# The order of two transpose groups and two output products in a gated delta net with experts

## The chip, the cores and the metric

The kernel runs on one core of one Trainium2 chip. The metric is the device time of the whole program in microseconds, from the start of the program to its end. The core's engines are TensorE (PE in the profile, with its weight loads on a row of their own, PEld), VectorE (DVE), ScalarE (ACT), GpSimd (POOL) and SyncE (SP), which only issues transfers here. Each engine works through its own instructions in the order in which they stand. An instruction that needs another engine's result waits on a semaphore, and whatever stands behind it on the same engine waits too.

## What is computed

The reference is one block of a transformer: attention by a gated delta rule, and then a mixture of experts. The change touches the attention part only, and of that its end:

```python
mixed_qkvz = einsum('bsd,od->bso', x, W_qkvz)            # projection: q, k, v, z
qkv = silu(conv_4(concat(q, k, v)))                      # causal convolution, 4 taps
# per chunk of 64 tokens, 32 value heads of 128 features:
M = tril(k_beta @ k.T * decay, -1);  T = inv(eye + M)
attn = (q @ k.T) * decay;  v_new = T @ v_beta - (T @ k_cumdecay) @ state
core = (q * exp(g)) @ state + attn @ v_new;  state = ...
h = core * rsqrt(mean(core ** 2) + eps)
h = norm_w * h * silu(z)
out = einsum('bsf,df->bsd', h, W_out)                    # the output product
x = x + layernorm(out)
# then 32 routed and 2 shared experts on layernorm(x), top 6 per token
```

There are 4 sequences of 256 tokens with 256 features, 16 query and key heads, 32 value heads. All values are 32-bit floats.

## The kernel before

**Units and turns.** The attention is cut into 32 units: one unit is one query/key head with its two value heads (R = 2) for two of the four sequences (512 tokens, four tiles of 128 rows). Every unit goes through the same stages, each a Python generator: `weights` and `decays` load and prepare, `prepare` projects (matmuls `pj`, line 390), convolves on ScalarE and VectorE (lines 398 and 400), squares the transposed q and k (`ptn`, lines 419 and 421) and forms the masked products of keys with keys and queries (`pk`, lines 442 and 461, scaled into the tile `am` by lines 446 and 464), `blocks` inverts small diagonal blocks on VectorE for two units at a time, `solve` combines them to the inverse by 64x64 products (lines 579, 640 and 648), `gate` makes the factor from z (line 364), and `finish` applies the inverse (`pu`), forms the output (`po`), normalises it on GpSimd (lines 709 and 711) and multiplies with the output weights.

**What sets the order.** Each `yield` of a generator names the place of the next step: `at(turn, slot)` is `turn * 9 + slot`, counted from the unit's own start, and unit u starts at turn u. A heap takes the step with the smallest place from all generators, and the order in which steps are taken is the order of the instructions on PE, ACT, DVE and POOL. So in one turn of the machine the first half of `prepare` of unit u, the second half of `prepare` of u-1, `solve` of u-2 to u-4 and `finish` of u-4 and u-5 are interleaved. SP is not in the list of engines ordered so: the recording layer orders its transfers itself.

**The end of `finish`.** For each half x (the first or the second 128 rows of the two sequences) four transposes turn `hm` into the PSUM tile `pth` (line 743), ScalarE copies it to `hT` (line 744), four products with the output weights `wo` sum into `pp` (line 749), and VectorE adds `pp` to the accumulator `acc` (line 754 for the first head, line 756 for the others). These steps stand in the same turn as the projections `pj` of the unit five later: `pj` number i of that unit stands at slot 2i + 0.7, so at 0.7, 2.7, 4.7 and 6.7. The step that multiplies two half inverses stands at slot 1.8 (`pyl`, line 640) and 3.7 (`pdl`, line 648, whose result line 650 copies to `phi` by two ScalarE instructions). The first level of `solve` of another unit (`py` and `pyx`, line 579) stands at 3.8.

**PSUM.** There are eight banks, two for each of four tags. `pj` has two of its own, `ms` is shared by `ptn`, `pk`, `ptv` and `pz`, `iv` by the products of `solve`, and `rc` by `pth`, `pp`, `pdl`, `pu`, `pm` and `po`. A tile that takes a bank waits for the last reader of the tile that had it.

A reader needs four names for a turn: `pth_0`, `pth_1` and `pp_0`, `pp_1` are the two halves' transposes and products; `pk_0`, `pk_1`, `pk_2` the three key products, of which `pk_1` takes the bank of `pk_0` and so waits for line 446 on it (called `am_0` below); `pj_0` to `pj_3` the projections. All matmuls but the transposes are recorded as two passes each.

Of the kernel before, what the change touches and what calls it, by code (L numbers as in the profile page):

```python
# [31 lines left out]
def at(turn, slot):  # L32
    return turn * SLOTS + slot
# [30 lines left out]
def gated_delta_net_moe(  # L64
# [26 lines left out]
    def bank(tag, shape, name):  # L91
        return psum.tile(shape, F32, tag=tag, name=name)
# [559 lines left out]
    def finish(u):  # L652

        hq, bp = units[u]
        yield at(4, 5)
        sz, vp, am, qe, phi = (state[u][k] for k in ("sz", "vp", "am", "qe", "phi"))
        vb = vp.rearrange("p (b x) r e -> p b x r e", x=2)
        ut = u1.tile([P, 2, 2, R, HD], F32, tag="ut", name=f"ut_{u}")
        rt = u1.tile([P, 2, R, HD], F32, tag="rt", name=f"rt_{u}")

        hm = u1.tile([P, 2, 2, R, HD], F32, tag="hm", name=f"hm_{u}")
        zb = sz.rearrange("p (b x) r e -> p x b r e", x=2)
        qx = qe.rearrange("p (b x) -> p x b", x=2)
        os_ = u2.tile([P, 2, 2, R], F32, tag="os", name=f"os_{u}")
        junk = u1.tile([P, HD], F32, tag="junk", name=f"junko_{u}")

        def solution(x):
            pu = bank("rc", [P, 2, R, HD], f"pu_{u}_{x}")
            for b in range(2):
                for r in range(R):  # L670
                    nc.tensor.matmul(  # L671
                        pu[:, b, r, :],
                        phi[:, r * NL + 2 * b + x, :],
                        rt[:, b, r, :] if x else vb[:, b, 0, r, :],
                        start=True,
                        stop=True,
                    )
            nc.scalar.copy(ut[:, x], pu)

        pos = {}  # L680

        def output(x):
            po = bank("rc", [P, 2, R, HD], f"po_{u}_{x}")
            for b in range(2):
                for r in range(R):
                    nc.tensor.matmul(  # L686
                        po[:, b, r, :], am[:, r, b, x, :], ut[:, 0, b, r, :], start=True, stop=(x == 0)
                    )
                    if x:
                        nc.tensor.matmul(  # L690
                            po[:, b, r, :], am[:, r, b, 4, :], ut[:, 1, b, r, :], start=False, stop=True
                        )
            for b in range(2):
                for r in range(R):
                    nc.scalar.activation(  # L695
                        junk, po[:, b, r, :], AF.Square, accum_out=os_[:, x, b, r : r + 1]
                    )
            pos[x] = po

        def gated(x):  # L700
            nc.vector.tensor_tensor(hm[:, x], pos[x], zb[:, x], ALU.mult)  # L701

        def normed(x):
            rs = u2.tile([P, 2, R], F32, tag="rs", bufs=4, name=f"rs_{u}_{x}")
            nc.vector.scalar_tensor_tensor(  # L705
                rs, os_[:, x], 1.0 / HD, qx[:, x].unsqueeze(2).to_broadcast([P, 2, R]), ALU.mult, ALU.add
            )
            rsf = rs.rearrange("p b r -> p (b r)")
            nc.gpsimd.tensor_tensor(rsf, rsf, nhalf[:, : 2 * R], ALU.pow)  # L709
            hf = hm[:, x].rearrange("p b r e -> p (b r) e")  # L710
            nc.gpsimd.tensor_tensor(hf, hf, rsf.unsqueeze(2).to_broadcast([P, 2 * R, HD]), ALU.mult)

        solution(0)
        yield at(4, 6)
        pm = bank("rc", [P, 2, R, HD], f"pm_{u}")
        for b in range(2):
            for r in range(R):
                nc.tensor.matmul(  # L718
                    pm[:, b, r, :], am[:, r, b, 3, :], ut[:, 0, b, r, :], start=True, stop=True
                )  # L720
        for b in range(2):
            nc.vector.tensor_tensor(rt[:, b], vb[:, b, 1], pm[:, b], ALU.subtract)
        yield at(4, 7)
        output(0)
        yield at(4, 7.45)
        gated(0)
        yield at(4, 8)
        solution(1)
        yield at(4, 8.2)
        normed(0)  # L730
        yield at(5, 0)
        output(1)
        yield at(5, 0.45)
        gated(1)
        yield at(5, 0.95)
        normed(1)
        for x in range(2):
            yield at(5, 1 + 2 * x)
            hT = u2.tile([P, 2, R, P], F32, tag="hT", name=f"hT_{u}_{x}")
            pt = bank("rc", [P, 2, R, P], f"pth_{u}_{x}")  # L740
            for b in range(2):
                for r in range(R):
                    nc.tensor.transpose(pt[:, b, r, :], hm[:, x, b, r, :], ident)
            nc.scalar.copy(hT, pt)  # L744
            yield at(5, 2.6 + 2 * x)
            pp = bank("rc", [P, 2, D], f"pp_{u}_{x}")
            for b in range(2):
                for r in range(R):
                    nc.tensor.matmul(  # L749
                        pp[:, b, :], hT[:, b, r, :], state[u]["wo"][:, r, :], start=(r == 0), stop=(r == R - 1)  # L750
                    )
            a = acc[:, bp * NL : (bp + 1) * NL, :].rearrange("p (b x) d -> p x b d", x=2)[:, x]
            if hq == 0:
                nc.vector.tensor_copy(a, pp)
            else:
                nc.vector.tensor_tensor(a, pp, a, ALU.add)
# [253 lines left out]
    for u in range(len(units)):  # L1010
        for stage in [weights, decays, prepare, gate, finish, solve] + [blocks] * (u % 2):
            begin(at(u, 0), stage(u))
# [57 lines left out]
```

## Time and profile before

| | us |
|---|---|
| median of 3 runs (1438.08 to 1443.58) | 1441.14 |
| the profiled execution's own time | 1443.05 |
| its span | 1441.3 |
| PE matmuls busy | 1353.2 (94%) |
| DVE busy | 872.6 (61%) |
| ACT busy | 852.3 (59%) |
| POOL busy | 554.6 (38%) |
| line 749, `pp`, 512 matmul records | 126.7 |
| line 743, `pth`, 256 records | 40.0 |

The span is that of one profiled execution, and it lies within the times of the runs. Busy time of PE is counted from records whose ends are modelled, so 94% does not say that the array is full for 94% of the time; what it loses is seen in the starts of the matmuls, and in the idle time of the weight-load row. Attention takes the span to about 1100 us; the rest is experts.

### The profile page before, as it was taken

To read this page: it belongs to the slowest core of one execution; us is meant where nothing else is said; L and a number is where in the kernel's file an instruction comes from. 1 tells how busy PE (TensorE), PEld (TensorE's weight loads), DVE (VectorE), ACT (ScalarE), POOL (GpSimd) and SP (SyncE) were. 2 spreads that over 40 slices of the span, in tenths; PEclk is the share of its full clock that TensorE was granted. 3 is DMA by queue.
4 is the path that set the end of the run, shared out by engine and by line. 5 is a ranking of instruction groups with operands and counts; after the bars stand their busy time and mean duration, and the time that the engine had idled before them with its cause. 6 is when DMAs were issued, how large, how long until landed. Compare 5 with 4: busy or idle time off the path is not lost.

```text
span 1441.3 us, 29913 instructions
## 1 busy us (share of the span) xinstructions
PE 1353.2 (94%) x11655; PEld 891.6 (62%) x11655; DVE 872.6 (61%) x1854; ACT 852.3 (59%) x2086; POOL 554.6 (38%) x430
## 2 busy tenths in 40 slices
PE   5668999999999999999999999999899999999996
PEld 3335766677777777777777677776665544444443
DVE  4576786878687687869879686877522242232122
ACT  3657778777777777777778677777443222122121
POOL 1353554566544556655544566545511100000000
PEclk8779999999999999999999999999999999999998
DMA  3344434334252433534242343533434565555621
GB/s 117 121 98 95 99 70 105 74 86 106 72 132 73 98 79 81 120 80 112 71 111 69 92 100 75 134 72 75 84 97 107 138 161 135 151 156 144 158 81 35
DMA packets 310157, 146.41 MB, mean 102 GB/s; under 512 B 240780, under 2 KB 281150, under 8 KB 310018
## 3 DMA queue, kind: packets, MB, share of 16 engines
q1 hardware_dynamic: 310018, 144.51, 40.9%
q8 instruction: 93, 1.52, 0.5%
q14 instruction: 46, 0.38, 0.1%
HBM read 129.40 MB, written 15.06 MB: 100 GB/s over the span
## 4 chain that ended last, share of the span: by engine, by line
PE 66%; DVE 14%; ACT 8%; DMA 7%; issue 3%; POOL 1%; SPq 0%; POOLq 0%; ACTq 0%; DVEq 0%
PE ph L922 11%; PE py L942 11%; PE pj L390 9%; PE pp L749 6%; PE pz L364 4%; DVE c L400 4%; DMA db<-dd 4%; PE pu L671 3%; PE pd L579 3%; DMA diag<-db 3%; PE po L686 3%; DVE prod L542 3%; ACT junk L421 2%; PE pk L461 2%; PE pm L718 2%
## 5 line engine op out<-in xcount | busy, mean ns | idle before, releaser
L400 DVE SCALAR_TENSOR_TENSOR c<-pj,cw,c 128x510 f32<-128x510 f32 (+2 forms) x384 | 286.1, 745 | 122.4 <-ACT c L398 113.3
L709 POOL TENSOR_TENSOR rs<-rs,nhalf 128x4 f32<-128x4 f32 x64 | 66.6, 1040 | 492.4 <-DVE rs L705 309.6
L390 PE MATMUL pj<-xT,w 128*128 128x512 f32 x512 | 250.3, 613 | 3.6 <-DVE c L400 3.4
L925 ACT ACTIVATE h<-ph,b1s 128x512 f32<-128x512 f32 (+1 forms) x94 | 64.6, 687 | 242.9 <-PE ph L922 242.7
L922 PE MATMUL ph<-xT,we 128*128 128x512 f32 (+1 forms) x376 | 177.4, 594 | 3.0 <-ACT phi L624 1.3
L931 DVE TENSOR_TENSOR hg<-h,gb 128x512 f32<-128x512 f32 (+1 forms) x94 | 65.0, 693 | 186.3 <-ACT h L925 169.8
L942 PE MATMUL py<-hg,we 128*128 128x512 f32 (+1 forms) x376 | 176.4, 593 | 0.0
L398 ACT ACTIVATE c<-pj,cw 128x512 f32<-128x512 f32 x128 | 87.6, 686 | 139.7 <-PE pj L390 139.5
L587 POOL TENSOR_TENSOR e<-am,cst 64x1024 f32<-64x1024 f32 x64 | 151.4, 2366 | 2.4
L390 PEld LDWEIGHTS pj<-xT,w 128*128 128x128 f32 x512 | 96.2, 198 | 77.8 <-issue 73.7
L749 PE MATMUL pp<-wo,hT 128*128 128x256 f32 x512 | 126.7, 391 | 7.3 <-ACT hT L744 4.6
L942 PEld LDWEIGHTS py<-hg,we 128*128 128x128 f32 (+1 forms) x376 | 71.3, 190 | 90.5 <-issue 89.1
L749 PEld LDWEIGHTS pp<-wo,hT 128*128 128x128 f32 x512 | 96.4, 193 | 45.0 <-ACT hT L744 30.5
L364 PE MATMUL pz<-wz,xT 128*128 128x256 f32 x512 | 121.2, 380 | 0.0
L922 PEld LDWEIGHTS ph<-xT,we 128*128 128x128 f32 (+1 forms) x376 | 69.6, 189 | 82.1 <-issue 78.1
L701 DVE TENSOR_TENSOR hm<-po,sz 128x512 f32<-128x512 f32 x64 | 43.7, 683 | 121.3 <-ACT junko L695 108.4
L346 POOL TENSOR_TENSOR gw<-gw,ng 128x512 f32<-128x512 f32 (+1 forms) x124 | 99.3, 832 | 2.4
L364 PEld LDWEIGHTS pz<-wz,xT 128*128 128x128 f32 x512 | 92.5, 190 | 10.5 <-issue 0.5
L191 POOL TENSOR_TENSOR rs_d<-rs_d,nhalf 128x2 f32<-128x2 f32 x4 | 2.8, 696 | 248.0 <-DVE rs_d L190 248.0
L446 DVE SCALAR_TENSOR_TENSOR am<-pk,br,gw 128x512 f32<-128x512 f32 x128 | 89.9, 744 | 6.7 <-ACT gw L338 4.8
L442 PE MATMUL pk<-c 128*128 128x512 f32 x128 | 74.6, 665 | 17.6 <-DVE am L446 10.5
L327 POOL TENSOR_TENSOR gw<-gw,cst 128x1024 f32<-128x1024 f32 x32 | 75.5, 2358 | 35.3 <-DMA gw<-g_rows 35.3
(188 smaller groups left out, 2768.7 us busy)
## 6 DMA issues: line engine op xcount, KB each, us to landing
gw<-g_rows SPq DMA_DIRECT2D x32, 768.0 KB, 6.5
w<-in_w_qkvz SPq DMA_DIRECT2D x32, 512.0 KB, 3.9
diag<-db SPq DMA_DIRECT2D x128, 128.0 KB, 3.4
we<-in_w SPq DMA_DIRECT2D x126, 128.0 KB, 3.0
gb<-gate_rows SPq DMA_DIRECT2D x34, 256.0 KB, 3.7
wz<-in_w_qkvz SPq DMA_DIRECT2D x32, 256.0 KB, 3.1
wo<-in_w_out SPq DMA_DIRECT2D x32, 256.0 KB, 2.7
mb<-am SPq DMA_DIRECT2D x64, 128.0 KB, 2.7
```

The source lines that it names most:

```text
L327: nc.gpsimd.tensor_tensor(gd, gd, neg.unsqueeze(1).unsqueeze(1).to_broadcast([P, 2 * R, 2, P]), ALU.add)
L346: nc.gpsimd.tensor_tensor(y, y, g.unsqueeze(2).to_broadcast([P, 2, n * P]), ALU.add)
L364: nc.tensor.matmul(pz[:, j].rearrange("p r e -> p (r e)"), xT[:, k, t * P : (t + 1) * P], state[u]["wz"][:, k, :], start=(k == 0), stop=(k ...
L390: nc.tensor.matmul(pj.rearrange("p b s -> p (b s)"), state[u]["w"][:, k, col * P : (col + 1) * P], xT[:, k, bp * T : (bp + 1) * T], start= ...
L398: nc.scalar.activation(y, pj, AF.Copy, scale=cw[:, row, 3:4])
L400: nc.vector.scalar_tensor_tensor(y[:, :, back:], pj[:, :, : S - back], cw[:, row, 3 - back : 4 - back], y[:, :, back:], ALU.mult, ALU.add,)
L442: nc.tensor.matmul(pk, s[:, 1, b * S : b * S + P], s[:, 0:2, b * S : (b + 1) * S], start=True, stop=True)
L446: nc.vector.scalar_tensor_tensor(am[:, r, b, 0:4, :].rearrange("p (i x) c -> p i (x c)", i=2), pk, br[:, 2 * b, r : r + 1], gw[:, r, b, 0: ...
L587: nc.gpsimd.tensor_tensor(e[g], mt[g, :, g].unsqueeze(1).to_broadcast(full), lev[g].unsqueeze(2).to_broadcast(full), ALU.mult,)
L749: nc.tensor.matmul(pp[:, b, :], hT[:, b, r, :], state[u]["wo"][:, r, :], start=(r == 0), stop=(r == R - 1))
L922: nc.tensor.matmul(ph[:rows], w[:, k * P : k * P + rows], xT[:, k, c], start=(k == 0), stop=(k == 1))
L942: nc.tensor.matmul(py[m], w[:rows, 2 * P + m * P : 2 * P + (m + 1) * P], hgs[i // 3][:rows, i % 3 * T : (i % 3 + 1) * T], start=False, sto ...
```

## The change

Two lines in `finish` change, both of them places.

```diff
         for x in range(2):
-            yield at(5, 1 + 2 * x)
+            yield at(5, 1 + 2.9 * x)
             hT = u2.tile([P, 2, R, P], F32, tag="hT", name=f"hT_{u}_{x}")
             pt = bank("rc", [P, 2, R, P], f"pth_{u}_{x}")
...
             nc.scalar.copy(hT, pt)
-            yield at(5, 2.6 + 2 * x)
+            yield at(5, 2.72 + 2.03 * x)
             pp = bank("rc", [P, 2, D], f"pp_{u}_{x}")
```

The first transposes stay at slot 1. The first product moves from 2.6 to 2.72, the second from 4.6 to 4.75; so each of them, with its addition to `acc`, stands behind the projection next to it (2.7 and 4.7) instead of ahead of it. The second transposes, with their copy, move from slot 3 to 3.9: behind `pdl` (3.7) and the first-level products `py` and `pyx` (3.8), and no longer ahead of `pk_1` (3.4). No instruction is added or taken away.

## The prediction

> **What bounds the kernel now.** I read the engines' shares first, then the waits, then one turn in order of time. The page says that TensorE is the busiest engine, and the chain that ended last runs mostly over it:
>
> ```profile
> PE 1353.2 (94%) x11655; PEld 891.6 (62%) x11655; DVE 872.6 (61%) x1854; ACT 852.3 (59%) x2086; POOL 554.6 (38%) x430
> PE 66%; DVE 14%; ACT 8%; DMA 7%; issue 3%; POOL 1%; SPq 0%; POOLq 0%; ACTq 0%; DVEq 0%
> ```
>
> The other third of the chain matters here: it passes through ACT and DVE at fixed places of each turn. The table of waits gives those near the change (total us, times, longest):
>
> ```profile
> PEld pp L749 <- ACT hT L744: 30.5, 30, 3.0
> PEld pdl L648 <- DVE acc L756: 17.4, 23, 0.8
> PEld pk L442 <- DVE am L446: 16.2, 27, 7.1
> PEld pth L743 <- POOL hm L711: 11.0, 29, 2.0
> PEld py L579 <- DMA diag<-db: 10.4, 15, 2.5
> ```
>
> So the moved instructions do wait in nearly every turn: products for their transposed operand, `pdl` for its bank (held by pp_0 until line 756 has read it), transposes for GpSimd, `pk_1` for am_0, and py for a transfer. A weight load runs one matmul ahead, so its idle time overstates what the array loses. That is read from one turn's order of time (start, duration, engine and line). ACT and DVE:
>
> ```profile
> 500.55 0.28 ACT L695 ACTIVATE junko<-po 128x128 f32<-128x128 f32 x1 [0.22 <-PE po L690]
> ...
> 503.61 0.68 ACT L398 ACTIVATE c<-pj,cw 128x512 f32<-128x512 f32 x1
> 504.19 0.58 ACT L744 COPY hT<-pth 128x512 f32<-128x512 f32 x1
> ...
> 511.37 0.75 ACT L650 COPY phi<-pdl 64x256 f32<-64x256 f32 x2 [0.17 <-PE pdl L648]
> ...
> 504.33 2.31 DVE L400 SCALAR_TENSOR_TENSOR c<-pj,cw,c 128x510 f32<-128x510 f32 x3 [1.49 <-ACT c L398]
> ...
> 507.23 0.86 DVE L643 TENSOR_SCALAR y_l<-pyl 64x256 f32<-64x256 f32 x2
> 508.12 1.41 DVE L446 SCALAR_TENSOR_TENSOR am<-pk,br,gw 128x512 f32<-128x512 f32 x2
> ```
>
> and TensorE, with the group at 509.58 being pk_1:
>
> ```profile
> 503.58 1.13 PE L442 MATMUL pk<-c 128*128 128x512 f32 x2
> 504.82 1.99 PE L749 MATMUL pp<-wo,hT 128*128 128x256 f32 x8
> 506.65 1.88 PE L390 MATMUL pj<-xT,w 128*128 128x512 f32 x4
> 508.37 0.60 PE L419 MATMUL ptn<-cst,c 128*128 128x128 f32 x4
> 508.97 0.66 PE L743 MATMUL pth<-cst,hm 128*128 128x128 f32 x4
> 509.58 1.13 PE L442 MATMUL pk<-c 128*128 128x512 f32 x2
> ```
>
> The reader is to see that pk_1 starts 0.05 us after am_0 ends (508.12 + 1.41 = 509.53), and that am_0 stands at the end of a chain without a hole: TensorE's po, ScalarE from 500.55 (four squares of po, four of ptn, the scaling at 503.61), VectorE from 504.33 to 509.53. Nothing in it comes from pth_0, pp_0 or pj_1. So **pk_1 is pinned** about 7.1 us behind pth_0, whatever TensorE does in between. This turn is typical: in 18 of the 23 turns from 280 us to 976 us pk_1 starts 7.13 to 7.15 us behind pth_0, and later in the others.
>
> **The change part by part.** The streaming times are the start-to-start distances of the trace: pk_0 takes 2 x 0.43 = 0.86 us, a pj group 4 x 0.43 = 1.72, a pp group 8 x 0.216 = 1.73, four transposes 0.44 and about 0.09 more where the kind of work changes.
>
> *The first product behind the projection.* Before, pk_0 has streamed by 503.58 + 0.86 = 504.44 and pp_0 starts at 504.82, because the copy of hT ends at 504.77: 0.38 us lost, some 0.28 of it more than a change of work costs. After, pj_1 fills that hole (504.45 to 506.17), pp_0 runs 506.17 to 508.0. This stall goes. What is late next: ptn_0 (to 508.45) and then pk_1, which still starts at 509.58. The 0.28 us, the 0.15 us that pth_1 waits for GpSimd and the 0.1 us of wait ahead of pk_1 are swallowed by the pin. **Gain up to pk_1: nothing.**
>
> *The second transposes behind pk_1.* They used 0.53 us of the time ahead of the pin, which was needed by nothing else. They now stand behind it, where TensorE has no spare time: before, from 509.58 to the next unit's pu at 516.13, its groups follow one another with only the 0.2 us hole ahead of pdl. **Cost: +0.53 us a turn.** TensorE now idles 508.45 to 509.58 instead.
>
> *pdl no longer waits for line 756.* In the built program pdl takes the bank of pth_0, free by 504.77, so it starts when pk_1 has streamed, 509.58 + 0.86 = 510.45 instead of 510.64: **-0.2 us a turn.**
>
> *A new wait.* In the built program pth_1 is given the very bank that pdl used just before it, and its first transpose waits for ScalarE too, where before it waited for TensorE and GpSimd alone. The releaser is line 650. Its two copies end 512.12 - 510.64 = 1.48 us after pdl's start, so after the change at 510.45 + 1.48 = 511.93. TensorE arrives earlier: pdl, py and pyx took 511.72 - 510.64 = 1.08 us, so 511.53. **Cost: +0.45 us** in turns like this one. ScalarE is free for line 650 in time: ptn_0 ends 0.4 us earlier than before, so the squares are done by about 510.4. Queued behind pth_1 on TensorE are pk_2, pj_2, pp_1 and pu, and the whole next turn. In the other turns (every second one) py waits 0.3 to 0.5 us for the diag transfer, whose landing does not move; there TensorE arrives about when line 650 ends, and the new wait costs about nothing.
>
> This is the place to weigh a rule. The row is 511.37 with 0.75 us for line 650. The Trainium skill, page "Perfetto Trace Analysis", section "Matmuls", says that independent matmul groups should go round different PSUM banks so that one's evacuation runs beside the next one's matmuls. pdl and pth_1 are independent and share a bank now; the rule speaks against this change. By the rule kept (other bank) a turn would cost 0.53 - 0.2 = +0.33 us; by the row +0.8. I take the row.
>
> *The second product behind the projection.* hT for it is ready: pth_1 ends about 512.5, the copy takes 0.58, and pk_2 (0.96) and pj_2 (1.72) come first. Before, py, pyx and pk_2 covered it as well. Zero either way; without that cover, the copy with its latency would cost about 0.8 us. VectorE does the same work in another order (the convolution of pj_1 ahead of the addition) without an idle gap from 504.33 to 517, so it is neither sooner nor later at pk_1's and py's results. po later takes pp_1's bank: line 756 is done about 518, po starts after 520. Zero.
>
> *SP and POOL.* The order of transfers changes with it: the load of wo (line 307), which waited for pp_1 at the head of SP's queue (released at 514.64), now stands behind the two mb stores (0.63 us of issue each) and in every second turn behind gw (about 0.6 to 1.0 us). The mb stores were issued at 516.61, when line 464 had ended, so they gain nothing. wo is issued about 518.5 at the latest and lands 2.7 us later, at about 521.2; POOL's scaling of it (line 312) started at 520.36, so it may slip by 1 us; POOL then has about 8 us idle, and wo is first used in the next turn. The load of wm stands behind wo, needs about 519.9 and finds wo issued by then. Zero; uncovered it would be 1 us a turn.
>
> **Sum.** Turn as shown: pth_1 at 511.98, pk_2 512.5, pj_2 513.5, pp_1 515.2, pu 516.9 instead of 516.13: +0.8. Turns with the diag wait: 0.53 and little else, +0.55. From the first unit's output to the last projection there are some 28 turns: 14 x 0.8 + 14 x 0.55 = 18.9 us. In the last four, without projections to hide the copy, pth_1 stands nearer to pp_1: about 0.6 us each, 2.4 us. Sum 21 us. Against the span of 1441.3 this gives 1462.6; the median, 1441.14, lies by the span, so I say 1462 for it. After 1160 us the experts keep TensorE full, so a late start is not won back.
>
> **The rivals.**
>
> *Displacement alone* (16%): the copy of line 650 comes soon enough, or the diag wait is in all turns, and only 0.33 us a turn remain: 29 x 0.33 = 10, so 1451. For it: the new wait is a difference of two times of about a microsecond. Against: the rows above.
>
> *A second circuit* (9%): pp_1 and its addition come 2.5 us later than before, and if VectorE's addition then holds up line 722 or po, or ScalarE (copy, silu, table load and exponentials in a row from 512.4) delays the convolution by 0.6 us, a turn costs 1.4: 28 x 1.4 = 39, so 1480. For it: ScalarE's row is dense there. Against: TensorE arrives later too.
>
> *Faster* (6%): pk_1 isn't pinned. If the chain to am_0 gains from TensorE's later turns, so that pk_1 follows ptn_0 at once (508.5), and TensorE doesn't wait for line 650, a turn gains 1.1 - 0.33 = 0.75: 28 x 0.75 = 21, so 1420. It decides from the point where am_0 ends 0.33 us earlier relative to pth_0 (0.8 if line 650 holds). Against: ScalarE waits 0.22 us for po at 500.55, so the chain starts from TensorE itself and moves with it.
>
> *No difference* (8%): the sum of pin and displacement cancels, for instance where GpSimd is late for pth_1 (2.0 us at the longest) and the later place hides it: 1441 to 1448.
>
> **How the numbers follow.** My case has 61%, alone within 1455 to 1472. Within 0.5% (7.2 us, about what a measurement of this kernel can tell from no change) lies only the fourth rival: 8%. Slower: 61 + 16 + 9 = 86%. Faster: 6%. The range leaves out the faster rival, most of no difference and the far end of the second circuit: 1448 to 1479.
>
> **What would show it.** Right: pp no longer waits for hT in most turns; pth waits for line 650 some 14 to 25 times, 0.4 us or more each; pdl no longer waits for line 756; pk's wait for line 446 rises to about 1 us a turn; a turn is 0.5 to 0.8 us longer between pk_1 and pu, and equal between pth_0 and pk_1. Wrong: pk_1 less than 6.9 us behind pth_0, or turns lengthened anywhere else.

## The result, and the profile after

The changed kernel takes 1467.79 us (median of 5 runs, 1462.45 to 1469.04) where the kernel before takes 1441.35 (5 runs, 1438.08 to 1444.46). The ratio is 1.0171, with an interval of 1.0152 to 1.0190: slower by 26 us, where 21 were forecast, and inside the range. The profiled execution took 1468.96 us. From its page, the span, the engines' shares and the chain that ended last:

```profile
span 1466.8 us, 29860 instructions
...
PE 1351.3 (92%) x11655; PEld 900.6 (61%) x11655; DVE 874.5 (60%) x1854; ACT 853.0 (58%) x2086; POOL 554.7 (38%) x430
...
PE 66%; DVE 11%; ACT 9%; POOL 7%; issue 3%; DMA 3%; SPq 0%; POOLq 0%; ACTq 0%; DVEq 0%
```

The matmuls, VectorE, ScalarE and GpSimd are as busy as before, to within 2 us; 25.5 us of span were added beside that. Where it waits is in the table of waits of the changed kernel (total us, times, longest; rows between are left out):

```profile
ACT phi L650 <- PE pdl L648: 43.8, 32, 3.1
PEld pk L442 <- DVE am L446: 43.7, 27, 7.5
PE pk L442 <- DVE am L446: 37.3, 27, 7.3
PEld pdl L648 <- issue: 21.1, 29, 0.8
PE pth L743 <- POOL gw L327: 6.4, 15, 0.4
PEld pp L749 <- ACT hT L744: 6.2, 6, 2.1
```

The products' wait for hT has gone from 30.5 us to 6.2, as the change intends. In its place TensorE's wait ahead of pk for line 446 has risen to 37.3 us in 27 waits. Before, its row was this:

```profile
PE pk L442 <- DVE am L446: 10.5, 7, 6.8
```

In both kernels one long wait (6.8 and 7.3 us) lies far ahead of the first output. After, the other 26 are pk_1's, in 26 of the 28 turns from the first output to the last projection; in the remaining two pk_1 waits for ScalarE's squares. pth has a wait in 15 turns. `pdl` is no longer booked to line 756, yet its weight load loses 21.1 us to "issue": the hole stayed, and only its name changed.

The turn that the prediction followed, in order of time (start, duration, engine, line; count; idle time before and its releaser). It starts with pth_0 at 510.29; the rows of `pyl`, `py` and `pyx`, and other rows of DVE and ACT, are left out:

```profile
510.29 0.60 PE L743 MATMUL pth<-cst,hm 128*128 128x128 f32 x4
511.43 1.13 PE L442 MATMUL pk<-c 128*128 128x512 f32 x2
512.40 1.88 PE L390 MATMUL pj<-xT,w 128*128 128x512 f32 x4
514.11 1.89 PE L749 MATMUL pp<-wo,hT 128*128 128x256 f32 x8
515.84 0.60 PE L419 MATMUL ptn<-cst,c 128*128 128x128 f32 x4
515.98 1.41 DVE L446 SCALAR_TENSOR_TENSOR am<-pk,br,gw 128x512 f32<-128x512 f32 x2
517.44 1.13 PE L442 MATMUL pk<-c 128*128 128x512 f32 x2 [1.00 <-DVE am L446]
518.50 0.51 PE L648 MATMUL pdl<-phi,y_l 64*64 64x64 f32 x10
519.22 0.75 ACT L650 COPY phi<-pdl 64x256 f32<-64x256 f32 x2 [1.12 <-PE pdl L648]
520.07 0.63 PE L743 MATMUL pth<-cst,hm 128*128 128x128 f32 x4 [0.43 <-POOL gw L327]
520.53 1.03 PE L461 MATMUL pk<-c 128*128 128x256 f32 x4
521.40 1.88 PE L390 MATMUL pj<-xT,w 128*128 128x512 f32 x4
523.12 1.89 PE L749 MATMUL pp<-wo,hT 128*128 128x256 f32 x8
524.84 1.05 PE L671 MATMUL pu<-vp,phi 128*128 128x128 f32 x8
```

The first projection (512.40) does fill the hole that pp_0 left, and TensorE is done with everything ahead of pk_1 at 516.4. It then idles for 1.00 us, because am_0 ends at 517.39, as pinned as before. Behind pk_1 stands what used to be ahead of it: pth_1, and in front of that 0.43 us of wait. The profile books the wait to GpSimd's line 327; but the two copies of line 650, which hold the bank that pth_1 takes, end at 519.22 + 0.75 = 519.97, and pth_1 starts 0.10 us later. It is a wait for several semaphores, and the engine named is not the one that matters. Measured from pth_0, in us, in a regular turn (before without the diag wait / with it; after the same in both kinds):

| | pk_1 | pdl | pth_1 | pk_2 | pp_1 | pu |
|---|---|---|---|---|---|---|
| before | 7.14 | 8.20 | 6.52 | 9.28 / 9.6 to 9.8 | 10.24 / 10.5 to 10.8 | 13.69 / 14.0 to 14.2 |
| after | 7.15 | 8.20 | 9.78 | 10.24 | 12.82 | 14.55 |

So up to `pdl` nothing has moved, and the turn is 0.86 us longer, or 0.3 to 0.6 where the diag transfer used to be waited for. Of the 25.5 us, 21.2 lie in the 28 turns from the first pth_0 on (902.7 against 881.5 us), 1.4 in what follows, and 2.9 ahead of the first output.

Not all of this is waiting. The profile also gives the granted clock, the share of its full clock at which TensorE could run. In the table of stretches (length, busy us of PE, PEld, DVE, ACT, POOL with counts, granted clock, DMA share, GB/s) the stretch from 100 to 150 us reads, before and then after:

```profile
100.00:150.00 50.00, 44.93 (x537) 31.14 (x529) 33.27 (x72) 35.10 (x85) 20.00 (x14) 0.95 0.39 86
```

```profile
100.00:150.00 50.00, 45.18 (x521) 32.37 (x514) 32.17 (x70) 33.32 (x71) 20.36 (x15) 0.88 0.34 87
```

No moved matmul has run by then, and TensorE's busy time is no less: its clock was granted at 0.88, not 0.95. The clock goes to half in pieces of some 3.4 us. From 112 to 1420 us the trace before has two of them (6.8 us in all), the trace after six and one of 10.2 us (30.7 in all). Two of those, at 126 and 146 us, go with the 2.9 us ahead of the first output. Four more fall into the turns that begin at 216, 668, 804 and 871 us, which are 1.7 to 2.2 us longer than before, and the one of 10.2 us into the turn at 1055, which is 2.6 longer. The one in the turn at 804 (second line), and the corresponding place of the kernel before (first line):

```profile
798.00:804.00 6.00, 4.68 (x47) 3.69 (x48) 5.05 (x11) 3.18 (x3) 5.85 (x7) 1.00 0.49 108
```

```profile
815.20:818.60 3.40, 3.40 (x38) 3.01 (x39) 1.27 (x3) 1.30 (x2) 3.40 (x4) 0.50 0.50 111
```

That is not an accident of one execution: the mean granted clock is 0.969 to 0.975 in the five runs after (median 0.972), and 0.973 to 0.982 in the 126 runs of the kernel before that stand beside the experiments (median 0.978). Among those 126, a run with 0.001 less took 0.9 to 1.2 us longer, so I estimate that 5 to 7 of the 26 us come by way of the clock. The kernels below with the transposes displaced have medians of 0.972 to 0.974, the others 0.975 to 0.981. What lowers the clock was not tried apart.

### The profile page after: what moved, and what is told of

It reads as the page before. It is cut to its first block, busy times and chain, and to the rows that moved or that the text cites. A ratio compares the mean times of both kernels' runs of the same rounds, so it can differ in the third digit from the quotient of the medians.

```text
span 1466.8 us, 29860 instructions
## 1 busy us (share of the span) xinstructions
PE 1351.3 (92%) x11655; PEld 900.6 (61%) x11655; DVE 874.5 (60%) x1854; ACT 853.0 (58%) x2086; POOL 554.7 (38%) x430
## 4 chain that ended last, share of the span: by engine, by line
PE 66%; DVE 11%; ACT 9%; POOL 7%; issue 3%; DMA 3%; SPq 0%; POOLq 0%; ACTq 0%; DVEq 0%
PE ph L922 11%; PE py L942 11%; PE pj L390 8%; PE pz L364 6%; DVE c L400 5%; PE pp L749 4%; PE pu L671 4%; PE po L686 4%; PE pd L579 4%; ACT junk L421 3%; POOL gw L327 3%; ACT junko L695 2%; PE pm L718 2%; PE pk L461 2%; PE po L690 2%
## 5 line engine op out<-in xcount | busy, mean ns | idle before, releaser
L749 PE MATMUL pp<-wo,hT 128*128 128x256 f32 x512 | 123.3, 384 | 3.6 <-ACT hT L744 3.6
L442 PE MATMUL pk<-c 128*128 128x512 f32 x128 | 75.0, 669 | 44.8 <-DVE am L446 37.3
L421 ACT ACTIVATE junk<-ptn 128x128 f32<-128x128 f32 x256 | 71.0, 277 | 49.3 <-PE ptn L419 42.2
L364 PEld LDWEIGHTS pz<-wz,xT 128*128 128x128 f32 x512 | 92.5, 190 | 10.5 <-issue 0.5
```

The source lines that it names most:

```text
L364: nc.tensor.matmul(pz[:, j].rearrange("p r e -> p (r e)"), xT[:, k, t * P : (t + 1) * P], state[u]["wz"][:, k, :], start=(k == 0), stop=(k ...
L421: nc.scalar.activation(junk, pt[:, t, :], AF.Square, accum_out=ss[:, i, t : t + 1])
L442: nc.tensor.matmul(pk, s[:, 1, b * S : b * S + P], s[:, 0:2, b * S : (b + 1) * S], start=True, stop=True)
L749: nc.tensor.matmul(pp[:, b, :], hT[:, b, r, :], state[u]["wo"][:, r, :], start=(r == 0), stop=(r == R - 1))
```

## The experiments

Each was timed in three rounds beside the kernel before (medians 1442.81 to 1443.74 us in those runs), so ratios are compared. "Behind pth_0" is read as in the table above. All compute the whole result.

**Each half of the change alone.** First the transposes alone:

```diff
-            yield at(5, 1 + 2 * x)
+            yield at(5, 1 + 2.9 * x)
```

> Only the second transposes move (slot 3 to 3.9); both products stay ahead of their projections. Theory of the pin: pk_1 stays about 7.1 us behind pth_0, since its bank comes free with line 446, and the transposes' 0.5 us are added behind it; here pth_1 takes the bank of pp_0 and need not wait for line 650, so a turn gets about 0.45 us longer and the run is 10 to 18 us above the kernel before: 1451 to 1459. Rival, that the products' new places cost the time: no more than 3 us above the kernel before. Rival, that the bank shared with pdl is the whole of it: also near the kernel before.

Measured: 1461.88 us (1459.86 to 1464.94), ratio 1.0126 [1.0095, 1.0157]; 3 us above what was expected. pk_1 stays at 7.14, pdl at 8.20, pth_1 stands at 9.28 (it waits for no bank here) and pu at 14.15, +0.46. The displacement alone brings the largest part of the loss. In its profile the 26 turns from the first pth_0 on took 16.9 us more than before; 8.6 of that lie in three turns in which the clock is at half for 3.4 or 6.8 us, and those had not been counted on.

Then the products alone:

```diff
-            yield at(5, 2.6 + 2 * x)
+            yield at(5, 2.72 + 2.03 * x)
```

> Only the two products move behind their projections; the second transposes stay at slot 3. Theory of the pin: the removed wait of pp_0 for its transposes (some 0.3 us a turn) gains nothing, because pk_1 still starts 7.1 us behind pth_0; pdl now takes the bank of pth_1 and may wait about 0.3 us for its copy: 1441 to 1449, not faster. Rival, that the removed wait is worth its own length: 27 x 0.3 = 8 us faster, 1433. Rival, that the products' places cost the time of the change: about 1462 to 1468.

Measured: 1448.02 us (1445.51 to 1454.82), ratio 1.0038 [1.0025, 1.0051]. The wait that the change aims at is gone and nothing was gained for it; the kernel is some 5 us slower. From the table of waits of this kernel:

```profile
PEld pp L749 <- ACT hT L744: 4.9, 4, 2.1
PEld pdl L648 <- ACT hT L744: 22.3, 25, 1.2
PEld pth L743 <- POOL hm L711: 22.2, 30, 2.0
```

pp_0 moves to 3.82 (from 2.38) and pk_1 stays at 7.14: the time goes into pth_1's wait for GpSimd, which grew from 11.0 to 22.2 us and is swallowed by the pin too. Here `pdl` takes another bank and waits for a copy of hT, 0.14 us longer than it waited before, and pu is at 13.83.

**The bank.** The changed kernel, with pth_1 in a bank of the projections, so that it shares none with `pdl` (in the units 0 to 25):

```diff
-            pt = bank("rc", [P, 2, R, P], f"pth_{u}_{x}")
+            pt = bank("pj" if x and u < 26 else "rc", [P, 2, R, P], f"pth_{u}_{x}")
```

> The changed kernel with the second transposes of the units 0 to 25 in a bank of the projections, so that they don't wait for line 650's copies of pdl. Theory: pth_1 starts right behind py and pyx, about 9.3 instead of 9.8 us behind pth_0 in turns without a wait for the diag transfer, 9.5 to 9.6 in the others: 0.2 to 0.5 us a turn, 6 to 12 us faster than the changed kernel, 1456 to 1462, and still 15 us or more above the kernel before, because the displaced transposes remain. Rival, that the shared bank is the whole loss: about 1443. Rival, that the bank costs nothing since the transfer would be waited for anyway: 1466 to 1469.

Measured: 1459.54 us (1458.01 to 1459.84), ratio 1.0106 [1.0078, 1.0134], about 9 us less than the changed kernel. Its timeline in the same turn (pth_0 at 505.80):

```profile
512.94 1.12 PE L442 MATMUL pk<-c 128*128 128x512 f32 x2 [1.00 <-DVE am L446]
...
514.73 0.75 ACT L650 COPY phi<-pdl 64x256 f32<-64x256 f32 x2 [1.12 <-PE pdl L648]
...
515.08 0.65 PE L743 MATMUL pth<-cst,hm 128*128 128x128 f32 x4
```

pth_1 starts at 9.28 while line 650 is still at work until 515.48, with no idle time in front of it. So the releaser was line 650, whatever the wait was booked to, and the wait cost 0.5 us in the turn. pk_1's 1.00 us of idling is as in the changed kernel, and the displaced transposes still stand behind it: the turn is 31.03 us, 0.39 longer than before. Of the rest of this kernel's loss, part is again in turns with the clock at half (three, 7.3 us).

**The pin.** The changed kernel, with the scaling of pj_0 (line 398) ahead of ScalarE's four squares of ptn_1, so that am_0's chain no longer holds these squares (about 0.4 us each), and TensorE's work is the same:

```diff
                 nc.tensor.transpose(pt[:, t, :], s[:, i, t * P : (t + 1) * P], ident)
+            if i:
+                yield at(1, 0.72)
             for t in range(NL):
...
-        squares(1)
+        yield from squares(1)
```

(and the same for the call of `squares(0)`, which yields nothing.)

> The changed kernel with ScalarE's scaling of pj_0 (line 398) ahead of its four squares of ptn_1 instead of behind them, so that VectorE's chain to am_0 begins about 0.9 us earlier. Theory of the pin: pk_1 starts about 6.2 instead of 7.15 us behind pth_0, and the turn gets up to 0.9 us shorter where nothing else holds it (where the diag transfer lands late, about 0.2): 12 to 22 us faster than the changed kernel, 1446 to 1456. Rival, that pk_1's start isn't what limits the turn: within 4 us of the changed kernel, 1464 to 1470.

Measured: 1450.02 us (1446.18 to 1453.24), ratio 1.0040 [1.0028, 1.0052]: a gain of 19 us, where the loss was 26, from an edit that touches no instruction of the change. Its timeline (lines are up to 2 further down; pth_0 at 503.55):

```profile
503.75 0.69 ACT L398 ACTIVATE c<-pj,cw 128x512 f32<-128x512 f32 x1 [0.53 <-PE pj L390]
...
508.26 1.41 DVE L448 SCALAR_TENSOR_TENSOR am<-pk,br,gw 128x512 f32<-128x512 f32 x2
...
509.73 1.12 PE L444 MATMUL pk<-c 128*128 128x512 f32 x2
```

The scaling now waits only for its projection and starts 0.20 us behind pth_0. am_0 starts 4.71 us behind pth_0 rather than 5.69 and ends at 509.67; pk_1 follows at 6.18 rather than 7.15, with no idle time of the array in its row. That is the pin: ScalarE's order sets the place of pk_1, and TensorE's order cannot.

Both repairs together (the two edits above on the changed kernel):

> The changed kernel with both repairs: the second transposes in a bank of their own and the scaling of pj_0 ahead of the squares. Theory: the two losses, pin and bank, are of different places and their repairs mostly add up (8 and 18 us alone): 1437 to 1446, at the kernel before. Rival: they are one loss, and both repairs together give no more than the larger alone, 1450.

Measured: 1442.77 us (1440.33 to 1448.63), ratio 0.9988 [0.9973, 1.0003]. The two gains, 9 and 19 us, add up to the loss. They do not undo it place by place: the regular turn is 30.06 us, where it was 30.64 before, the turns with the diag wait 31.0 to 31.5 rather than some 31.0, and the clock stays at 0.973. The earlier scaling alone on the kernel before was not run, so how much it would have gained there is not known. The nearest pair, with the products ahead of their projections and py moved in both, is at the end of the next part (before_py and before_early_py): there it brings 0.33%, about 5 us, and pk_1 does not come earlier (7.30 rather than 7.14). So I take most of the 19 us to be a matter of the changed order.

**The gain behind the pin.** If the products' place is good and only the pin hides it, it should show once the pin is lifted. First the products' move without its cost on VectorE: in it, line 756 stands behind the convolution, and here it is kept ahead of it.

```diff
             nc.scalar.activation(y, pj, AF.Copy, scale=cw[:, row, 3:4])
+            yield at(0, 2 * i + 0.76)
             for back in range(1, 4):
...
-            yield at(5, 2.6 + 2 * x)
+            yield at(5, 2.72 + 2.03 * x)
```

> Both products stand behind their projections on TensorE, the second transposes stay at slot 3, and VectorE keeps the old order (the addition of pp ahead of the convolution of the projection next to it), so that the banks go round as before and no new wait appears. Theory of the pin: the wait of pp_0 for its transposes (0.3 us a turn) is gone from the waits, pk_1 still starts 7.1 us behind pth_0, and the time stays that of the kernel before: 1438 to 1446. Rival, that the removed wait is worth its length once no new wait comes with it: 8 us faster, near 1435.

Measured: 1446.83 us (1443.71 to 1450.07), ratio 1.0027 [1.0017, 1.0037], just above the expected range. pdl is back at 8.20 and pu at 13.68 as before, in the regular turns. The profiled execution loses its 4 us in a few others: some with the clock at half (in the one with pu at 19.16 it is so for 6.8 us), some in which py waits longer for the diag transfer. With the pin in place, no gain.

The same with the earlier scaling:

> The kernel split with ScalarE's scaling of pj_0 ahead of its squares of ptn_1. Theory of the pin: am_0 ends 0.9 us earlier, pk_1 now starts when TensorE gets to it, about 6.6 us behind pth_0, and the removed wait counts: up to 0.5 us a turn, less where the diag transfer is waited for, 5 to 13 us faster than the kernel before, 1430 to 1438. Rival: TensorE's other work holds the turn anyway, 1440 to 1445.

Measured: 1439.00 us (1433.68 to 1445.53), ratio 0.9974 [0.9962, 0.9986], a little above the expected range. pk_1 is at 6.42 and pu at 12.86, but only in every second turn; in the others the diag transfer, which lands no earlier, now holds up py and all that stands behind it, and pu is mostly at 13.6 to 14.4.

So py and pyx were moved behind pk_2 as well:

```diff
-            yield at(3, 3.8 + 4 * i)
+            yield at(3, 3.8 + 4 * i) if i else at(3, 4.45)
```

> The kernel split_early with the first-level products of solve (py and pyx) behind pk_2 (slot 4.45 instead of 3.8), so that pk_2's 0.9 us lie before the wait for the diag transfer. Theory: the turns with that wait gain too, 0.5 us in nearly every turn, 10 to 20 us faster than the kernel before, 1424 to 1434. Rival: VectorE, which now does the sums of py and pyx behind the scaling of pk_2, is late for the next products, 1436 or more.

Measured: **1425.75 us** (1424.67 to 1427.38), ratio 0.9880 [0.9858, 0.9901]: faster than both kernels. Its timeline (lines up to 3 further down; pth_0 at 490.81):

```profile
496.79 0.60 PE L746 MATMUL pth<-cst,hm 128*128 128x128 f32 x4
497.23 1.02 PE L445 MATMUL pk<-c 128*128 128x512 f32 x2
498.19 0.68 PE L651 MATMUL pdl<-phi,y_l 64*64 64x64 f32 x16
498.80 1.13 PE L464 MATMUL pk<-c 128*128 128x256 f32 x4
```

The groups follow one another with no idle time from the transposes on; pk_2 is at 7.99 and pu at 13.22, or at 13.38 in the other turns. Of the 15.9 us of span gained, 10.7 lie in the 28 turns and 6.2 ahead of the first output, less about 1 lost behind them. The clock, 0.979, is as before.

Two kernels tell what the edits bring singly. The last edit alone on the kernel before:

> The kernel before with the first-level products py and pyx behind pk_2, nothing else. Theory: only the turns that wait for the diag transfer gain, by up to that wait (0.3 to 0.5 us in every second turn), since pk_1 stays 7.1 us behind pth_0 in all of them: 3 to 7 us faster than the kernel before, 1436 to 1440. Rival, that this step alone makes the 17 us of split_early_py: near 1426.

Measured: 1446.58 us (1443.36 to 1448.72), ratio 1.0022 [1.0014, 1.0029]: a miss. Its timeline:

```profile
508.17 0.68 PE L648 MATMUL pdl<-phi,y_l 64*64 64x64 f32 x16
508.78 1.13 PE L461 MATMUL pk<-c 128*128 128x256 f32 x4
...
510.46 1.99 PE L749 MATMUL pp<-wo,hT 128*128 128x256 f32 x8
```

The diag wait is hidden and all regular turns have the same length, but that is pu at 14.05, not 13.69. pdl takes 0.61 us up to pk_2, and py and pyx another 0.6 between pk_2 and pp_1, where the three together took 1.08 with their records overlapping (8.20 to 9.28). Parting them costs some 0.35 us with the change back, in every turn.

And the earlier scaling with that edit, but with the products at their old places:

> The kernel split_early_py with the products ahead of their projections again, as in the kernel before: the scaling of pj_0 ahead of the squares, py behind pk_2. Theory: the copy of the first transposes now stands 0.7 us later on ScalarE, and pp_0, with nothing ahead of it to hide that, waits 0.7 us longer; pk_1 starts about 7.6 us behind pth_0 though am_0 is done by 6.2, and the run is 5 to 12 us slower than the kernel before, 1446 to 1455. Rival, that the products' order does not matter here either: near split_early_py, 1426 to 1430.

Measured: 1440.86 us (1438.01 to 1443.39), ratio 0.9989 [0.9981, 0.9998], outside the expected range and better: pk_1 is at 7.30, since TensorE itself is now late (pp_0 waits for hT until 2.88), and pu at 14.10. The kernel of 1425.75 us differs from this one in the products' place and in VectorE's order alone, and is 15 us faster at the same clock (0.979): behind the projections the products do gain, once the pin is lifted.

Last, py kept next to pdl, both behind pk_2, to save the 0.35 us (the kernel of 1425.75 us, with this):

```diff
-        yield at(4, 3.7)
+        yield at(4, 4.44)
```

> The kernel split_early_py with pdl moved behind pk_2 as well (slot 4.44), so that pdl and the first-level products py and pyx stand next to each other again, as in the kernel before. Explanation under test: moving py alone behind pk_2 cost 0.35 us in every turn because two groups of 64x64 products that stood together were parted. If so, that comes back, and pk_1 to pu is 0.3 to 0.4 us shorter than in split_early_py: 27 x 0.35 = 9 us, 1414 to 1421. Rival: the 0.35 us belong to pk_2's new neighbours whatever stands there, 1424 to 1428.

Measured: 1431.18 us (1429.35 to 1432.91), ratio 0.9921 [0.9894, 0.9948]: a miss, slower than with them parted. From its timeline:

```profile
530.36 1.12 PE L445 MATMUL pk<-c 128*128 128x512 f32 x2
531.75 1.13 PE L464 MATMUL pk<-c 128*128 128x256 f32 x4 [0.27 <-ACT junk L424]
```

pdl, py and pyx do take 1.08 us together again. But pk_2, now directly behind pk_1, comes too early for its bank, which ScalarE's squares still read, and from pk_1 to pp_1 the turn takes 5.40 us rather than 5.07. So the 0.35 us are shown by before_py alone, and whether they belong to the parting or to pk_2's new neighbours stays open.

## Why the prediction was right

The mechanism was right and one term was not. The closeness of the sum is in part chance, since the clock, which no term has, made up for turns that did not lengthen.

*The first product.* Right. The stall went (hT: 30.5 to 6.2 us) and pk_1 did not move (7.14 to 7.15). p_only and split show no gain, and early_c shows what holds pk_1.

*The second transposes.* Right in kind. Alone they moved pk_2 by 0.49 us (9.28 to 9.77), where +0.53 was taken.

*pdl without its wait: -0.2 us.* **This step failed.** pk_1 to pdl takes 1.05 us with the wait booked to line 756, and 1.05 without it. pdl did not wait for line 756 even before. The two rows, VectorE's and TensorE's:

```profile
509.45 0.68 DVE L756 TENSOR_TENSOR acc<-pp,acc 128x512 f32<-128x512 f32 x1
```

```profile
510.64 0.51 PE L648 MATMUL pdl<-phi,y_l 64*64 64x64 f32 x10
```

Line 756 ends at 510.13, when pk_1 was still streaming by the prediction's own sum (to 510.45). Half of the 0.2 was my slip: I took pdl to start when pk_1 has streamed, after 0.86 us, and forgot the 0.09 that I had myself set for a change of work. The other 0.1 us lies inside pk_1, and the traces show what it goes with. Where pk_1 follows the transposes without a hole (in 22 turns of before_early_py and 9 of the kernel of 1425.75 us), its second pass starts 0.43 us behind its first. In the other 25 turns of these two, in all 28 of the kernel before and in all 28 after, it is 0.53 us, whether the hole was some 0.05 us or over 1. pk_1 comes behind a hole in both kernels, so nothing came back. The turn paid for it: pth_1 stands 9.78 behind pth_0, where 9.54 was forecast; smaller roundings further down took most of it back, so that the turn is +0.86, not +0.8.

*The new wait.* Right in place and cause, and in size in the regular turns: 0.43 us in the turn shown, where 0.45 was forecast, and 9 us of the total by own_bank. The matmul row has 15 such waits booked to GpSimd and 5, of 0.19 to 0.43 us, booked to "issue", where 14 to 25 were expected. In the turns with the diag wait the change cost 0.3 to 0.6 us, where 0.55 was taken; but the new wait is not nothing there, as was said: all turns now have pth_1 at 9.78, and with the bank changed such turns take 31.1 to 31.5 us rather than 31.5. The rule that was weighed, on different banks for independent groups, is borne out here: with it kept, in own_bank, a regular turn costs +0.39 us, where +0.33 was worked out, and without it +0.86, where the row gave +0.8.

*The second product, and SP and POOL.* No wait of pp on GpSimd's scaling of wo stands in the table of waits, and pp_1's wait for hT is gone from the turns. Zero, as said.

*The sum.* 18.9 us was forecast for 28 turns, 0.675 each on the average, and 21.2 came. Fifteen ordinary turns took 10.9, 0.72 each, near the forecast. Seven turns that were already long before, held up by late operands or transfers or by the clock, took 0.7 together, where the forecast counted 4.7. Four turns with the clock at half took 8.3, and the last two 1.3. The prediction had named turns lengthened elsewhere as a sign of being wrong. The waits stand where it put them, but the excess of these four turns, and the 2.9 us ahead of the first output, go with the clock, which no step had. The tail took 1.4 for 2.4, and there too the clock is in it.

*The rivals.* Displacement alone (1451) is what own_bank ran, and it took 15 us over before, not 10, though its regular turn, +0.39, is near the 0.33; the wait for the bank did decide against it. The second circuit is not seen in the regular turns, where ScalarE waits for pdl ahead of line 650. The faster rival needed am_0 to end earlier relative to pth_0; it took early_c's edit to do that.

## What to carry to other kernels

Before a stall is priced as a gain, look at the next instruction on that engine which waits for another one: if its releaser ends a chain that does not pass through the stall, everything ahead of it is free, and so is the stall. Work moved from ahead of such a pin to behind it costs its full length, and a tile that moves may be handed another bank, so look up who read that bank last. Shorten the pinning chain first, and then reorder: the same move of the products cost 0.3% with the pin (before and split) and gained about 1% without it (before_early_py and split_early_py, both with py moved). And compare the granted clocks before a difference in time is put down to waits alone.

## What the runs showed of the hardware that was not expected

Products of 64x64 of different groups overlap in the records when they stand next to each other: pdl, py and pyx take 1.08 us together, but 0.61 and 0.62 when they are parted, and with pk_2 between them the turn is some 0.35 us longer. A hole can outlive the wait that it was booked to: pdl's 0.8 us idle time of the weight load was put down to line 756 before (17.4 us in 23 turns) and to "issue" after (21.1 us in 29), with pdl at the same place. pk_1, of two passes, has its second pass 0.53 us behind the first where it starts behind a hole, and 0.43 where it does not; how long the hole was made no difference. And a wait for several semaphores was booked to GpSimd, while changing the bank alone, that is ScalarE's part of it, removed it.

The granted clock fell to half behind thin stretches, without a pause as long as the 3.4 us of its pieces. In the thirteen traces, from 112 to 1400 us, every fall from the full clock came behind 3.4 us of which TensorE's records filled 64% or less, mostly with holes of 0.3 to 2.3 us; no fuller stretch was followed by one, and every one under 47% was. Between those shares it went both ways: ahead of 125 us both kernels' records fill 47% of the stretch, and only the changed kernel's clock fell. No run changed the holes alone, so this is what stands side by side, and not a cause shown.
